# From attention's last out products to the mixer: text order on all engines, the last tile's scores first, a bank for the mask, and tiles taken one at a time

## The chip, the cores and the metric

The kernel runs on one core of a Trainium2 chip. A core has a matrix engine (TensorE, PE in the profile), a vector engine (VectorE, DVE), a scalar engine (ScalarE, ACT), a general engine (GpSimd, POOL) and a queue that issues transfers (SyncE, SP). Each engine works through its own list of instructions in the order in which the program was built, and waits at an instruction until the semaphores named there have been counted up by others. PE writes its results into PSUM, which has eight banks; all else lies in SBUF. The metric is the time of one execution on the device in microseconds (us).

## The reference, cut to what matters

One hybrid layer over x, 4 sequences of 256 positions with 512 channels, that is 1024 rows, in fp32. Four blocks are added to x one after the other, each of which reads a layer-normalised x:

```
x = x + attention(layernorm(x))   # 32 heads of 16, causal, rotary, an adapter prefix
x = x + ffn(layernorm(x))
x = x + mixer(layernorm(x))       # state space: 128 heads of 64, 8 groups
x = x + ffn(layernorm(x))

def ffn(x):                                   # 64 centroids, one assigned to each of 512 outputs
    dots = softmax(x @ centroids.T / 0.1)
    hits = dots > 0.01
    query_sel = any(hits, axis=1)             # by row
    row_sel = any(hits, axis=0)[assignments]  # by output column, over all rows
    return where(query_sel[:, None] & row_sel[None, :], x @ weight.T + bias, 0)

def mixer(x):
    gate, xBC, dt = split(x @ in_proj_w.T)
    xBC = silu(causal_conv(xBC) + conv_b)     # four taps
    y = chunked_scan(xBC, softplus(dt + dt_bias), A, D)
    return (group_rmsnorm(y * silu(gate)) * norm_w) @ out_w.T
```

Which columns the feed-forward adds (`row_sel`) is known only after the last of the eight tiles of 128 rows has its scores; the mixer's normalisation reads x after that.

## The kernel before

x stays in SBUF as eight tiles of 128 rows and 512 channels. Every fp32 product is made of three passes over split operands (`mm3`, lines 110 to 117: high by high, high by low, low by high); a split is a copy on ACT and a subtract on DVE or POOL (L107 and L108). A product of one tile with 512 channels thus takes 4 x 3 passes.

Attention runs tile by tile over four sequences (B = 4), 8 steps of four heads each. Its PSUM pools have 3 (`ps`, all-purpose), 4 (`ps_s`, scores) and 1 bank (`ps_y`). From step 23 on the first feed-forward (`Feed`, lines 175 to 268) is woven in: `fed` normalises a tile, turns it (four PE transposes L166, the split) and multiplies it with the centroids and weights in two halves of 288 columns (`products`); `choice` then makes the hits (max L230, scale L231, exp L233, reciprocal L235, hit L237, running maximum of hits L239), the row's selector `sel` (L243), and the new row (two bias adds L252, then L255, which multiplies by `sel` and adds x).

The attention loop is written in PE's order (`manual_schedule` for PE alone, line 703). On ACT, DVE and POOL a scheduler places the instructions by its own costs. After the last head step the out products of tiles 6 and 7 (`projected_out`, 12 passes of 512 columns each) are made; `finished` adds them to x, takes statistics (L138, L139) and the root (L143, L144). Tiles 6 and 7 are normalised, turned and fed (lines 784 to 806); tile 5's products come between the out products and tile 6's turn.

The mixer begins with `feed.select` (L258): a count product over all hits (L260, L261), a threshold on DVE (L263), a product with the assignment's one-hot (L264) that leaves the mask in PSUM. Then `take` (L268) copies the new row into x where the mask is set, tile by tile. Lines 902 to 929 work in pairs of tiles: two takes, two statistics, one root and one shift (L148) for both, two scalings on ACT (`scale_there`, L153, tile `mxn`), two turns (L166) with splits into `mx` (ACT L107, DVE L108). `normalised(p)` issues for PE: the first quarter of pair p-1, the turns of pair p, the second quarter of pair p-1. A quarter is the product of 256 rows with one weight block: `quarter(0, p)` with the dt weights into `first[0]`, `quarter(1, p)` with the first block of the input projection into `first[1]`. Here too the scheduler places the instructions, except those that are kept in program order (`keep_in_program_order`, the `pin` argument). Two products of x with ones (`warmed`, L122) stand among them on PE.

POOL makes three lower halves of weight splits in this stretch (L108 for `wd` and twice `w`). SP fetches the weights of the projections (`fetch`, L836), and waits there for the splits that free their buffers.

`opening` then makes the step sizes: `dv` (L960) reads `first[0]`, the first convolution (`conv`, L1022) reads `first[1]`, and from there on all engines but SP run in text order (line 1550) for the rest of the kernel: 64 blocks of the mixer, the output products and the second feed-forward.

## Time and profile before

| | |
|---|---|
| median of three runs | 1845.56 us (1845.04, 1845.56, 1850.23) |
| the profiled execution: its time | 1848.5 us |
| its span, first to last instruction | 1846.7 us |
| PE busy | 1779.6 us (96%), 12906 matmuls |
| DVE busy | 1427.2 us (77%) |
| ACT busy | 1283.2 us (69%) |
| POOL busy | 245.5 us (13%) |
| mean granted PE clock | 0.988 |
| first out product of tiles 6 and 7 | 339.83 us |
| first take | 361.80 us |
| `dv`, the first reader of the step sizes' product | 388.37 us |

The profile shows one execution. Busy times of matmuls overlap, because matmuls are pipelined, so PE's 96% is not the share of its peak. A timeline row gives start and length in us, the engine, the line of the program, the operation and out<-in. The chain of work that ended last is followed back from the last instruction, at each step to what released it. The window table gives the busy time of each engine in a stretch, with the number of instructions behind it, in the order PE, weight loads, DVE, ACT, POOL, then the granted PE clock, the share of the transfer engines and GB/s.

### The profile page before, as it was taken

Reading aid. Unit: us, or ns where it says so; the run is one execution under the profiler, and the core shown is the slowest. Engines: PE = TensorE matmul, PEld = TensorE weight load, DVE = VectorE, ACT = ScalarE, POOL = GpSimd, SP = SyncE. Lnnn points to the kernel's source line nnn. Section 1 sums busy time; section 2 is a strip of 40 time slices with the busy share of each in tenths; the row PEclk is TensorE's granted clock in tenths of the full one; section 3 lists DMA queues with packets and bytes.
Section 4 is the critical chain, followed back from the end, with each engine's and each line's share of the span. In section 5 each row is a group of like instructions: output and inputs, shape, how many; then the busy total and the mean of one; then the engine's idle time right before and its main releaser. Section 6 shows DMA issues by size and latency. Waiting matters only on the chain.

```text
span 1846.7 us, 33141 instructions
## 1 busy us (share of the span) xinstructions
PE 1779.6 (96%) x12906; PEld 1451.8 (79%) x12906; DVE 1427.2 (77%) x2152; ACT 1283.2 (69%) x2536; POOL 245.5 (13%) x253
## 2 busy tenths in 40 slices
PE   8999988899999999999999999999999999999988
PEld 6777767677877888888888888888888888888877
DVE  5566667678988777878877787879787878887777
ACT  6666666367778667766866686668667866767664
POOL 6332330000110111101101110110111011101100
PEclk9999989999999999999999999999999999999999
DMA  4000000112325333433442343225333433343321
GB/s 146 1 1 1 23 15 5 47 58 85 103 92 164 100 101 110 133 104 92 131 133 81 108 155 98 98 86 161 96 99 104 154 103 92 114 134 114 96 79 55
DMA packets 134237, 169.45 MB, mean 92 GB/s; under 512 B 12224, under 2 KB 77376, under 8 KB 134080
## 3 DMA queue, kind: packets, MB, share of 16 engines
q1 hardware_dynamic: 125008, 134.30, 24.0%
q10 hardware_dynamic: 9072, 33.03, 4.7%
q8 instruction: 101, 1.65, 0.4%
q14 instruction: 56, 0.46, 0.1%
HBM read 131.64 MB, written 35.65 MB: 91 GB/s over the span
## 4 chain that ended last, share of the span: by engine, by line
PE 79%; ACT 9%; DVE 8%; issue 2%; POOL 1%; DMA 1%; SPq 0%; ACTq 0%; DVEq 0%; POOLq 0%
PE pp L115 13%; PE pp L116 12%; PE pp L117 12%; PE pyy L1145 7%; PE pog L117 6%; PE pog L115 6%; PE pog L116 6%; PE trx L1126 3%; ACT e L502 2%; DVE acc L1033 1%; PE ptr L518 1%; ACT em L1106 1%; PE pq L115 1%; PE pg L1063 1%; PE pq L116 1%
## 5 line engine op out<-in xcount | busy, mean ns | idle before, releaser
L115 PE MATMUL pp<-mx,w 128*128 128x512 f32 (+1 forms) x1160 | 463.6, 400 | 6.9 <-DVE acc L1033 6.2
L117 PE MATMUL pp<-mx,w 128*128 128x512 f32 (+1 forms) x1160 | 452.0, 390 | 0.0
L116 PE MATMUL pp<-mx,w 128*128 128x512 f32 (+1 forms) x1160 | 451.4, 389 | 0.0
L1178 POOL TENSOR_TENSOR sq<-sq,x 128x1024 f32<-128x1024 f32 x54 | 129.8, 2405 | 1204.0 <-ACT x L1177 1204.0
L115 PEld LDWEIGHTS pp<-mx,w 128*128 128x128 f32 x1160 | 218.4, 188 | 52.5 <-issue 7.0
L117 PEld LDWEIGHTS pp<-mx,w 128*128 128x128 f32 x1160 | 218.3, 188 | 46.7 <-DVE w L855 1.2
L116 PEld LDWEIGHTS pp<-mx,w 128*128 128x128 f32 x1160 | 218.7, 189 | 40.7
L1033 DVE SCALAR_TENSOR_TENSOR acc<-pp,cw_s,acc 128x1012 f32<-128x1012 f32 (+2 forms) x192 | 244.7, 1274 | 6.1 <-ACT acc L1022 1.6
L1119 DVE TENSOR_TENSOR em<-em,gm 128x1280 f32<-128x1280 f32 x128 | 189.4, 1489 | 75.3 <-ACT em L1114 75.3
L117 PE MATMUL pog<-wo,gh 128*128 128x512 f32 x512 | 200.1, 391 | 4.2 <-DVE gh L1245 4.2
L115 PE MATMUL pog<-wo,gh 128*128 128x512 f32 x512 | 200.5, 392 | 0.4 <-DVE x L1262 0.4
L116 PE MATMUL pog<-wo,gh 128*128 128x512 f32 x512 | 199.4, 389 | 0.0
L1129 DVE TENSOR_TENSOR xd<-trx,dt_t 128x512 f32<-128x512 f32 x128 | 82.4, 686 | 150.9 <-PE trx L1126 150.9
L1045 ACT ACT_TABLE_LOAD x63 | 80.8, 1283 | 154.6 <-DVE acc L1033 154.5
L1324 ACT ACTIVATE gt<-pp 128x1024 f32<-128x1024 f32 x64 | 65.6, 1026 | 154.2 <-PE pp L117 154.0
L1145 PEld LDWEIGHTS pyy<-em,xd 64*64 64x64 f32 x4096 | 131.7, 135 | 46.2 <-issue 16.9
L1145 PE MATMUL pyy<-em,xd 64*64 64x256 f32 (+3 forms) x4096 | 160.1, 304 | 4.3 <-DVE em L1119 4.3
L1106 ACT ACTIVATE em<-r,end_t 128x128 f32<-128x128 f32 x512 | 163.0, 389 | 0.8
L502 ACT ACTIVATE e<-sc,nmx 128x256 f32<-128x256 f32 (+1 forms) x256 | 104.2, 442 | 21.0 <-DVE nmx L496 20.9
L117 PEld LDWEIGHTS pog<-wo,gh 128*128 128x128 f32 x512 | 96.1, 188 | 26.8 <-DVE gh L1245 6.8
L115 PEld LDWEIGHTS pog<-wo,gh 128*128 128x128 f32 x512 | 96.2, 188 | 20.1 <-issue 0.8
L116 PEld LDWEIGHTS pog<-wo,gh 128*128 128x128 f32 x512 | 96.1, 188 | 19.5
(297 smaller groups left out, 3199.1 us busy)
## 6 DMA issues: line engine op xcount, KB each, us to landing
wr<-in_win_dram SPq DMA_DIRECT2D x144, 256.0 KB, 2.7
r<-cumd SPq DMA_DIRECT2D x256, 128.0 KB, 2.9
spill<-gb ACTq DMA_DIRECT2D x63, 512.0 KB, 3.2
gr<-spill SPq DMA_DIRECT2D x120, 256.0 KB, 3.4
wor<-in_wout_dram SPq DMA_DIRECT2D x64, 256.0 KB, 4.3
out_dram<-x SPq DMA_DIRECT2D x8, 256.0 KB, 2.2
x<-in_x_dram SPq DMA_DIRECT2D x1, 1536.0 KB, 8.8
gr<-spill SPq DMA_DIRECT2D x8, 192.0 KB, 2.5
```

Source lines behind the costliest of these rows:

```text
L115: nc.tensor.matmul(o, lh, rh, start=(first and k == 0), stop=False)
L116: nc.tensor.matmul(o, lh, rl, start=False, stop=False)
L117: nc.tensor.matmul(o, ll, rh, start=False, stop=(last and k == n - 1))
L502: nc.scalar.activation(es_[c][:, 2 * j + pr, :], sc[:, j, :], AF.Exp, bias=nm[:, j : j + 1], accum_out=rs[:, c, h : h + 1],)
L1033: nc.vector.scalar_tensor_tensor(av[:, :, d:], pv[:, :, : L - d], cw_s[:, ch, tap : tap + 1], av[:, :, d:], ALU.mult, ALU.add,)
L1045: nc.scalar.activation(pair(x2).rearrange("p k u i -> p u k i"), acc.rearrange("p (u k i) -> p u k i", u=2, i=Q), AF.Silu,)
L1106: nc.scalar.activation(piece(e, j, c, 2 - c, 2), rv[:, j, 2:, :], AF.Exp, bias=end_t[:, 2 * j + c, h : h + 1],)
L1119: nc.vector.tensor_tensor(e, e, gm, ALU.mult)
L1129: nc.vector.tensor_tensor(xd[:, hs, :].rearrange("p c (h d) -> p c h d", h=2), tr.rearrange("p c (h d) -> p c h d", h=2), dt_t[:, hs, 2 * ...
L1145: nc.tensor.matmul(py[d, u, j * L + c * Q : (j + 1) * L].rearrange("p (k i) -> p k i", i=Q), xd[us, 4 * j + c, d], piece(es2[hh], j, c)[us ...
L1178: (nc.gpsimd if n < NB - 2 else nc.vector).tensor_tensor(sqs[g], sqs[g], x2, ALU.add)
L1324: nc.scalar.activation(gts[i], pp, AF.Silu)
```

## The change

The last two out products go into a new pool of five banks (`f_c`); attention's own PSUM pools are closed ahead of it. The general pool of the mixer (`m_m`, two banks) is opened there already, and one bank (`f_k`) is set apart for the mask; the mixer's two-bank pool `m_y` is opened later for it. From these out products on PE, ACT, DVE and POOL all run in text order, to the end of the kernel.

Tile 5's turn stands ahead of the out products on PE, as before; its products move behind tile 6's turn. Tile 7's first half is split: 64 score columns first, then (behind the mask's products) the other 224 columns and the second half. The square-root table is loaded early by a one-element activation (`primed`), four small products with ones follow the last of PE's fed products, and the two on x go. `select` moves from the mixer to the place after tile 7's hits. The rest of `choice` for tiles 6 and 7 (bias adds, `sel`, L255 of before) is written behind it, and ahead of the first take.

The pairs of tiles are replaced by a loop over single tiles: take and statistics of tile t, root, shift and scaling of tile t-1, turn of tile t-2, and, from t = 4 on, one quarter. There are eight roots and shifts instead of five, and the pins of the pair loop go. The diff, with changes of indentation left out:

```diff
-    def attention(later):
+    def attention(later, region):
         with ExitStack() as es:
-            inner = ExitStack()
+            inner, banks = ExitStack(), ExitStack()
             pool = lambda name, bufs, **kw: es.enter_context(tc.tile_pool(name=name, bufs=bufs, **kw))
...
             p3 = pool("a3", 3)
-            ps = pool("a_m", 3, space=PSUM)
-            ps_s = pool("a_s", 4, space=PSUM)
-            ps_y = pool("a_y", 1, space=PSUM)
+            ps, ps_s, ps_y = (
+                banks.enter_context(tc.tile_pool(name=name, bufs=bufs, space=PSUM))
+                for name, bufs in (("a_m", 3), ("a_s", 4), ("a_y", 1))
+            )
...
-            def projected_out(b, c):
-                po = ps.tile([P, C], F32, name="po", tag="m")
+            def projected_out(b, c, where=None):
+                po = (where or ps).tile([P, C], F32, name="po", tag="c" if where else "m")
                 cs = slice(c * P, (c + 1) * P)
...
                 step("long", n + 2)
-                moved(fed(feed, 5), n)
                 step("turn", n + 2)
-                pos = [projected_out(b, c) for c in range(2)]
-                xns, xss = {}, {}
-                for c, po in enumerate(pos):
-                    t = 2 * b + c
-                    rooted = finished(b, c, po)
+                xs5 = normed(feed.norm, 5)
+                assert not nexts, nexts
+            banks.close()
+            freed = {"reuse_waits": "tile"}
+            mask_at = later.enter_context(tc.tile_pool(name="f_k", bufs=1, space=PSUM, side="right", **freed))
+            ps = ctx.enter_context(tc.tile_pool(name="m_m", bufs=2, space=PSUM, **freed))
+            region.enter_context(tc.manual_schedule(
+                engines={e.engine for e in (nc.tensor, nc.scalar, nc.vector, nc.gpsimd)}
+            ))
+            with tc.tile_pool(name="f_c", bufs=5, space=PSUM, **freed) as ps_c:
+                pos = [projected_out(b, c, ps_c) for c in range(2)]
+                xns, xss, halves = {}, {5: xs5}, {}
+                def added(t):
+                    nc.vector.tensor_tensor(x[:, t, :], x[:, t, :], pos[t - 6], ALU.add)
+                    feed.norm.stats(t)
+                def scaled(t):
+                    feed.norm.root(t, t + 1)
                     xns[t] = p2.tile([P, C], F32, name="axn", tag="t1")
...
-                def turned_late(t):
+                def turned_over(t):
                     tr = ps.tile([P, KC, P], F32, name="tr", tag="m")
-                    xss[t] = [p2.tile([P, KC, P], F32R, name=f"axs{j}", tag=f"axs{j}") for j in range(2)]
-                    feed.norm.turn(xns[t], tr, xss[t])
+                    xss[t] = xs = [
+                        p2.tile([P, KC, P], F32R, name=f"axs{j}", tag=f"axs{j}") for j in range(2)
+                    ]
+                    for k in range(KC):
+                        nc.tensor.transpose(tr[:, k, :], xns[t][:, k * P : (k + 1) * P], ident)
+                    nc.scalar.copy(xs[0], tr)
+                    return lambda: nc.vector.tensor_tensor(xs[1], tr, xs[0].bitcast(F32), ALU.subtract)
-                with tc.issue_after(rooted):
-                    step("long", n + 3)
-                turned_late(TT - 2)
-                halves = {t: [ps_s.tile([P, FH], F32, name="pd", tag="sc") for _ in range(2)] for t in xns}
-                feed.products(xss[TT - 2], 0, halves[TT - 2][0])
-                turned_late(TT - 1)
-                feed.products(xss[TT - 2], 1, halves[TT - 2][1])
-                feed.chosen(TT - 2, halves[TT - 2])
-                feed.tile(TT - 1, xss[TT - 1], halves[TT - 1])
-                assert not nexts, nexts
-            return feed
+                def products(t, j, cols=slice(0, FH)):
+                    if (t, j) not in halves:
+                        halves[t, j] = ps_c.tile([P, FH], F32, name="pd", tag="c")
+                    feed.products(xss[t], j, halves[t, j], cols)
+                added(6)
+                scaled(6)
+                lower = turned_over(6)
+                added(7)
+                lower()
+                scaled(7)
+                primed(AF.Exp)
+                products(5, 0)
+                products(5, 1)
+                c5 = feed.choice(5, [halves[5, j] for j in range(2)])
+                next(c5)
+                lower = turned_over(7)
+                products(6, 0)
+                next(c5)
+                lower()
+                next(c5)
+                next(c5)
+                products(6, 1)
+                products(7, 0, slice(0, NCL))
+                c6 = feed.choice(6, [halves[6, j] for j in range(2)])
+                next(c6)
+                next(c5)
+                halves[7, 1] = ps_c.tile([P, FH], F32, name="pd", tag="c")
+                c7 = feed.choice(7, [halves[7, j] for j in range(2)])
+                next(c7)
+                next(c6)
+                next(c7)
+                primed(AF.Sqrt)
+                cnt = ps.tile([NCL, P], F32, name="cnt", tag="m")
+                feed.select(cnt, mask_at.tile([P, C], F32, name="msk"))
+                products(7, 0, slice(NCL, FH))
+                products(7, 1)
+                warmed(ps.tile([P, C], F32, name="warm", tag="m"), [ones] * 4)
+                for _ in c6:
+                    pass
+                for _ in c7:
+                    pass
+            return feed, ps
-    def mixer(feed, later):
+    def mixer(feed, ps, later):
         with ExitStack() as es, ExitStack() as inner:
...
             po_ = pool("mo", 2, **freed)
-            ps = pool("m_m", 2, space=PSUM, **freed)
             w1 = inside("m1", 1, **freed)
...
             es_y, es_p = ExitStack(), ExitStack()
-            ps_y = es_y.enter_context(tc.tile_pool(name="m_y", bufs=1, space=PSUM, side="right", **freed))
             ps_p = es_p.enter_context(tc.tile_pool(name="m_p", bufs=2, space=PSUM, **freed))
...
             mnorm = Norm("m")
-            feed.select(
-                ps.tile([NCL, P], F32, name="cnt", tag="m"),
-                ps_y.tile([P, B * L], F32, name="msk", tag="pyy")[:, :C],
-            )
             first = [ps_p.tile([P, NT], F32, name="pp", tag="pp") for _ in range(2)]
-            xns = {}
+            xns, parts_ = {}, {}
+            def quarter(j, p):
+                project((wd, pieces[0])[j], first[j], slice(p * L, (p + 1) * L))
-            def normalised(p):
-                quarter = lambda j, n: project((wd, pieces[0])[j], first[j], slice(n * L, (n + 1) * L))
-                if p > 0:
-                    quarter(0, p - 1)
-                if p < B:
-                    for t in (2 * p, 2 * p + 1):
+            for t in range(TT + 2):
+                if t < TT:
+                    feed.take(t)
+                    mnorm.stats(t)
+                if 1 <= t <= TT:
+                    mnorm.root(t - 1, t)
+                    mnorm.shift(t - 1, t)
+                    xns[t - 1] = po_.tile([P, C], F32, name="mxn", tag="wo0", bufs=GB)
+                    mnorm.scale_there(t - 1, xns[t - 1])
+                if t >= 2:
+                    n = t - 2
                         tr = ps.tile([P, KC, P], F32, name="tr", tag="m")
-                        mnorm.turn(xns.pop(t), tr, [v[:, :, t * P : (t + 1) * P] for v in xs])
-                if p > 0:
-                    quarter(1, p - 1)
-            for p in range(B):
-                pin = {"pin": tc.keep_in_program_order} if p else {}
-                ts = (2 * p, 2 * p + 1)
-                if p == 0:
-                    pin = {"pin": tc.keep_in_program_order}
-                    feed.take(0)
-                    mnorm.stats(0, **pin)
-                    feed.take(1, **pin)
-                    for t in ts:
-                        if t:
-                            mnorm.stats(t, **pin)
-                        mnorm.root(t, t + 1)
-                        mnorm.shift(t, t + 1)
-                        warmed(ps.tile([P, C], F32, name="warm", tag="m"), [x[:, t, :]])
-                else:
-                    for t in ts:
-                        feed.take(t, **pin)
-                    for t in ts:
-                        mnorm.stats(t, **pin)
-                    mnorm.root(2 * p, 2 * p + 2)
-                    mnorm.shift(2 * p, 2 * p + 2)
-                if p:
-                    normalised(p - 1)
-                for t in ts:
-                    xns[t] = po_.tile([P, C], F32, name="mxn", tag="wo0", bufs=GB)
-                    mnorm.scale_there(t, xns[t])
-            normalised(B - 1)
-            normalised(B)
+                    mnorm.turn(xns.pop(n), tr, [v[:, :, n * P : (n + 1) * P] for v in xs])
+                    if n >= 2:
+                        quarter(n % 2, n // 2 - 1)
+            for j in range(2):
+                quarter(j, B - 1)
             later.close()
+            ps_y = es_y.enter_context(tc.tile_pool(name="m_y", bufs=1, space=PSUM, side="right", **freed))
             p2 = inside("m2", 2, **freed)
...
-            with tc.manual_schedule(
-                engines={e.engine for e in (nc.tensor, nc.scalar, nc.vector, nc.gpsimd)}
-            ):
                 opening()
...
     later = ExitStack()
-    mixer(attention(later), later)
+    with ExitStack() as region:
+        mixer(*attention(later, region), later)
```

In the diff `opening()` and what follows it lie one level further left than before, and are otherwise the same.

## The prediction

> **What bounds the kernel now.** I read first the page's busy shares and its chain of work that ended last. TensorE (PE) is busy for 96% of the span and holds 79% of the chain, so nearly everywhere the end moves only with PE's work. The change touches one short stretch, from attention's last two out products (339.8 us) to the start of the mixer's step sizes (388.4 us), so I then read the chain, the timeline and the window table of that stretch alone. The chain, start and length in us:
>
> ```profile
> 360.74 0.26 DVE fc L263
> 361.00 0.88 DVE fx L255
> 361.88 0.65 DVE x L268
> ...
> 376.14 0.60 ACT mx L107
> 376.76 0.69 DVE mx L108
> ...
> 380.88 0.69 DVE mx L108
> ...
> 388.37 0.68 ACT dv L960
> ```
>
> The stretch is a relay, not a PE stage. The first take (the predicated copy, L268) follows the last fed tile, then pairs of tiles pass through VectorE (DVE), ScalarE (ACT), PE, ACT and DVE. At full clock one pair costs 380.88 - 376.76 = 4.1 us, two tiles overlapping. The timeline gives the price of each hop:
>
> ```profile
> 361.80 0.71 DVE L268 COPY_PREDICATED x<-msk,fx 128x512 f32<-128x512 uint32 x1
> 362.55 0.69 DVE L138 BATCH_NORM_STATS2 st<-x 128x6 f32<-128x512 f32 x1
> 363.28 0.18 DVE L139 BATCH_NORM_AGGREGATE mmv<-st 128x2 f32<-128x6 f32 x1
> ...
> 382.15 0.15 DVE L144 RECIPROCAL mrs<-mrs 128x2 f32<-128x2 f32 x1
> 382.34 0.16 DVE L148 SCALAR_TENSOR_TENSOR mmv<-mmv,mrs 128x2 f32<-128x2 f32 x1
> ```
>
> Take to statistics is 0.75, statistics to their merge 0.73, reciprocal to shift 0.19. The window table (PE's busy us in each stretch, and PEclk near the end of each row) shows the clock:
>
> ```profile
> 348.70:352.10 3.40, 1.55 (x11) 1.07 (x10) 2.68 (x10) 2.17 (x5) 0.00 (x0) 1.00 0.00 0
> 352.10:355.50 3.40, 3.40 (x17) 3.38 (x16) 1.33 (x5) 0.77 (x3) 0.00 (x0) 0.51 0.00 0
> ...
> 358.90:362.30 3.40, 2.17 (x15) 1.47 (x13) 2.81 (x9) 2.20 (x4) 1.27 (x1) 1.00 0.01 2
> ...
> 365.70:369.10 3.40, 1.21 (x8) 0.73 (x8) 3.31 (x6) 1.90 (x4) 1.18 (x1) 1.00 0.53 151
> 369.10:372.60 3.50, 2.74 (x11) 2.44 (x12) 3.49 (x10) 0.87 (x2) 0.00 (x0) 0.51 0.61 228
> 372.60:376.00 3.40, 3.40 (x18) 3.40 (x18) 0.94 (x3) 0.94 (x2) 0.00 (x0) 0.50 0.00 0
> ```
>
> A stretch with 1.2 to 1.6 us of PE work is followed by one at half clock; 2.17 us kept it full; 2.74 us at half clock did not win it back, 3.40 us did.
>
> **The change, part 1: out products to the first take.** The out products now write into the new pool of five banks. Their first bank is one whose last reader is the yT subtract on L108 (339.70 for 0.41), where PE now waits only for an L252 add that ends at 339.78: +0.3, start 340.15. Start to tile 6's residual add is 3.11 today (339.83 to 342.94), add to its normalised tile's end 2.75 (to 345.69); kept, they put tile 6's turn at 346.05. PE then has no wait: turn 0.44, tile 5's 24 products at 0.133, turn 0.44, tile 6's 24 products, tile 7's 12 score products at 0.111 (the feed-forward at the kernel's end has this shape: 1831.92, 1832.03): 8.6 us, to 354.66. Tile 7's turn is reached at 349.7 and its normalised tile is done near 349.0. This removes what PE loses today: 1.62 us idle before 350.95 and the half-clock row, about 13 products 0.107 us slower each.
>
> The gain is then spent. After the score products land (354.86) come max 0.26, scale 0.27, exp 0.44, reciprocal 0.20, hit 0.28: the second count product at 356.3, its threshold on DVE 0.42 later, mask product 0.34 later, 357.1. PE waits inside this and resumes at 357.4 with 12 products of 224 columns (0.111) and 12 of 288 (0.133): 2.9 us, the last landing at 360.5. On DVE the text puts tile 7's two bias adds and its product with sel ahead of the first take. So a mask ready at 357.5 is not used: bias add 0.50, sel product 0.68, first take 361.7. To this comes GpSimd (POOL). Its three weight splits, now behind an early square-root table load, run about 358 to 361.7, under that last product, which reads two SBUF tiles. Today such an operation takes 0.95 instead of 0.75 beside a split (360.93), and a shift 0.94 instead of 0.16 (365.95). I take +0.4, bounds 0 and 1.3 (one split is 1.27). First take 362.1 against 361.80: **+0.3**, bounds -0.1 and +1.2.
>
> **Part 2: tiles singly, in text order.** In one turn of the new loop DVE's queue holds take(t), statistics, merge, reciprocal and shift of t-1, and the subtract mx1 of t-2; ACT's holds the scaling mxn(t-1), then the copy mx0(t-2). DVE stands at mx1(t-2) for mx0(t-2), which stands on ACT behind mxn(t-1), which waits for DVE's shift(t-1). Behind the waiting subtract stand the next take, statistics and shift. So a turn is a ring: mx1 0.61, take 0.75, statistics 0.73, merge 0.10, reciprocal 0.19, shift to mxn 0.20 (382.34 to 382.54), mxn 0.71 (two in 1.52, 0.81 each), mx0 to mx1 0.62 (376.14 to 376.76): **3.9 us a tile, 7.8 a pair**, against 4.1 now. DVE idles about 1.3 of it.
>
> With T the first take: three takes, statistics and merges, two roots and shifts bring the second shift at T+5.2, the first mx1 at T+6.74 = 368.8 (368.64 now: no loss yet). Today's first pair then costs 8.1 us (368.64 to 376.76), because its products and turns run at half clock; two new turns cost 7.8. The other pairs lose 3.7 each. The sixth mx1 is at T+26.3 = 388.4; the last two tiles have no take in front, and the eighth mx1 comes near T+29.6 = 391.7 against 385.57 now. From the last subtract on the distance to dv is unchanged at full clock (first waiting product 386.31, dv 388.37), as PE does quarter (1, 2) in the meantime. Part 2 without the clock: 391.7 - 385.57 = 6.1, less the 0.3 of part 1: **+5.8**.
>
> Three roots and shifts more (about 0.3 each) lie within these turns. The two 1.1 us warm-up products on x go; four on ones, 0.27 each, stand behind tile 7's products and delay no turn, as the first is due at 366.5. The 12 extra instructions of tile 7's split cost 12 x (0.111 + 0.111 - 0.133) = 1.1 us of PE, counted above. POOL's 0.5 us fill moves behind the splits and nothing waits for it. SP issues the same transfers; the weight fetches that wait for the splits (361.36, 365.68) come 2 to 4 us sooner, and one output-weight fetch goes behind two of them. All had landed long before their readers, which come later now: nothing. The mask's own bank keeps no one waiting.
>
> **Part 3: the clock at the end of the ring.** From the warm-ups (361.5) to the first projection product (about 373) PE has only three turns, so the clock is halved then. Inside the ring one turn at half clock gives PE 12 x 0.213 + 0.8 = 3.4 of 3.9 us, 3.0 per 3.4 us stretch, between the 2.74 that stayed and the 3.40 that recovered. At full clock it gives 2.0, 1.75 per stretch, between the 1.55 that lost and the 2.17 that kept. I take half clock as the likelier, by the nearer row: 1.75 stands closer to 1.55. From 388.4 PE is loaded without a gap: quarter (0, 2), the last turn, then (1, 2), (0, 3), (1, 3). At half clock (0, 2) holds back the last turn by 12 x 0.093 = 1.1, the turn itself takes 0.4 more, and (1, 2) now lies in front of (0, 3). If the clock returns after four to five busy us, dv is **+1.9**; bounds 0 (full clock) and +4.7 (half to the end of (1, 3), where the conv waits).
>
> The Trainium skill's page "TensorE: Matmul & The Clock Gate", section "Why this matters for your kernels", asks for no idle gap over some 3 us, one idle window being what halves the clock. Here a gap of 1.62 us was enough (row 348.70). By the page the ring's 2 us gaps would keep a clock once regained and the sum would be near +6.1; I go by the row.
>
> **Sum.** 0.3 + 5.8 + 1.9 = +8.0 us at dv. From there ACT, DVE and PE follow in one chain, and nothing in the opening waits for anything that did not move (PE's next projection waits for dv itself), so the end moves by as much. The profiled execution took 1848.5 (span 1846.7), 2.9 above the median of the three runs, 1845.56 (1845.04 to 1850.23). Against itself the sum gives 1856.5; by the median, which I forecast, 1853.6.
>
> **Rivals.** (a) *The ring at full clock.* For it: 2.17 us a stretch kept the clock today. Against: 1.75 is less. 0.3 + 5.8 = +6.1: 1851.7. (b) *The head gains more.* If the half-clock row's whole loss (1.4) and the idle 1.62 came off the first take, with the clock as in the forecast: 8.0 - 0.3 - 3.0 = +4.7: 1850.3. Against: the DVE order puts tile 7's adds before the takes. (c) *Not slower: the hops overlap.* If ACT's copies didn't stand behind the scalings, DVE's own work would set the turn: 0.61 + 0.75 + 0.73 + 0.10 + 0.19 + 0.1 = 2.5 us. Five turns save 7.0, at full clock 6.1 - 7.0 = -0.9: 1844.7. It decides below about 2.7 us a turn. For it: the pair at 4.1. Against: both queues' written order. (d) *The change doesn't do what it says*: the mask is early, but no take profits; that lies in the forecast already.
>
> **How the numbers follow.** Forecast (+7 to +11) 0.60; (a) 0.21; (b) 0.11; (c) 0.05; 0.03 for something faster that I do not see. 0.3% is 5.5 us, about what a measurement of this kernel can tell from no change. Slower: 0.60, some 0.15 of (a), 0.04 of (b): 0.79. Same: 0.17. Faster: 0.04. The range takes in (a), the near part of (b), and half clock to the end with the lock (8.0 + 2.8 + 0.9 = +11.7 at most): 1849.8 to 1857.0.
>
> **What would show it.** Subtracts mx1 3.9 us apart, each with some 1.3 us of DVE idle ended by ACT's mx copy; ACT idle ended by the shift; the mask product near 357 and the first take near 362; PEclk near 0.5 after 366; dv near 396. It is wrong if the subtracts stand 2.5 apart, if the first take comes before 360, if PEclk stays at 1.0 through the ring (then rival (a)), or if the chain after dv is shorter than today.

## The result, and the profile after

The changed kernel takes 1858.30 us, median of five executions (1855.83 to 1860.56). The kernel before, on the same chip, now has a median of 1849.57 us over five. The ratio is 1.0053, 95% interval 1.0034 to 1.0072: slower by about half a per cent, 8.7 us between the medians. The profiled execution took 1855.83 us (span 1854.0), against 1848.5 (span 1846.7) for the profile before: 7.3 us.

The forecast was 1853.6, within 1849.8 to 1857.0. The direction and the ring came as told; the time lies above the range.

First the chain of waits of the changed kernel over the stretch (start, length, engine, tile, line):

```profile
360.43 1.47 DVE fx L255
361.89 0.65 DVE x L268
...
371.07 0.81 ACT mxn L153
371.88 0.48 ACT mx L107
...
372.38 0.69 DVE mx L108
373.08 0.65 DVE x L268
...
373.75 0.71 DVE st L138
...
374.93 0.82 ACT mxn L153
...
395.56 1.26 ACT dv L989 x2
```

Scaling, copy, subtract, take, statistics, then (left out here) merge, reciprocal and shift, then the next scaling: the same names come round turn after turn, each once per tile. That is the ring. The timeline shows one turn of it with what each engine waited for:

```profile
372.38 0.69 DVE L108 TENSOR_TENSOR mx<-tr,mx 128x512 fp32r<-128x512 f32 x1 [1.35 <-ACT mx L107]
...
372.99 0.72 DVE L268 COPY_PREDICATED x<-msk,fx 128x512 f32<-128x512 uint32 x1
...
374.74 0.16 DVE L148 SCALAR_TENSOR_TENSOR mmv<-mmv,mrs 128x1 f32<-128x1 f32 x1
...
374.93 0.82 ACT L153 ACTIVATE mxn<-x,mmv,mrs 128x512 f32<-128x512 f32 x1 [2.39 <-DVE mmv L148]
...
375.66 0.56 ACT L107 CAST mx<-tr 128x512 fp32r<-128x512 f32 x1
...
376.25 0.69 DVE L108 TENSOR_TENSOR mx<-tr,mx 128x512 fp32r<-128x512 f32 x1 [1.36 <-ACT mx L107]
```

From subtract to subtract 376.25 - 372.38 = 3.87 us. VectorE stands 1.35 of it, ended by ScalarE's copy; ScalarE stands 2.39, ended by VectorE's shift. Each waits for the other once a turn. In the list of who waited for whom the subtract's line reads (us in all, how often, longest):

```profile
DVE mx L108 <- ACT mx L107: 11.2, 8, 1.7
```

Before, the same wait came twice, 5.6 us in all. The window table (PE's busy us in each stretch first, PEclk as the third figure from the end):

```profile
362.30:365.70 3.40, 0.00 (x0) 0.00 (x0) 3.23 (x9) 0.69 (x2) 0.00 (x0) 0.92 0.84 281
365.70:369.10 3.40, 2.22 (x8) 1.44 (x8) 1.88 (x6) 2.08 (x5) 0.00 (x0) 0.50 0.28 109
...
372.60:376.00 3.40, 3.30 (x17) 2.94 (x16) 2.19 (x6) 1.07 (x2) 0.00 (x0) 0.59 0.00 0
376.00:379.40 3.40, 1.89 (x16) 1.69 (x15) 2.43 (x6) 0.99 (x3) 0.00 (x0) 1.00 0.02 5
...
386.20:389.60 3.40, 1.81 (x11) 1.56 (x12) 1.23 (x6) 2.19 (x4) 0.00 (x0) 0.92 0.00 0
389.60:393.00 3.40, 3.40 (x20) 3.40 (x20) 1.13 (x2) 1.16 (x3) 0.00 (x0) 0.58 0.00 0
```

The clock is halved when PE runs dry behind the head (the part from the out products to the first take). By the means of its rows, 0.59 and 0.92, it comes back near 375.4, holds for some 13 us with 1.8 to 2.4 us of work a stretch, and is lost again near 389, just where PE is loaded at last. So it is neither half all through the ring, as the forecast had it, nor full, as rival (a).

The stretch does not start at the same time in every trace, so all that follows is counted from the start of VectorE's yT subtract on L108, the last operation of attention's heads on VectorE ahead of the out products (339.70 before, 338.90 after). First subtract is the first mx1, last subtract the end of the eighth:

| kernel | first take | first subtract | end of last subtract | dv | time against before, 95% |
|---|---|---|---|---|---|
| before | 22.10 | 28.94 | 46.55 | 48.67 | |
| changed | 22.92 | 29.62 | 54.35 | 56.66 | 1.0053 (1.0034 to 1.0072) |
| changed, again (c1_after) | 22.92 | 29.62 | 53.10 | 55.22 | 1.0041 (1.0028 to 1.0054) |
| e1_order | 23.78 | 30.00 | 51.15 | 53.28 | 1.0036 (1.0024 to 1.0048) |
| e2_pairs | 24.96 | 32.96 | 47.46 | 50.92 | 1.0013 (1.0005 to 1.0022) |
| e3_warm | 23.75 | 30.48 | 54.86 | 56.98 | 1.0052 (1.0038 to 1.0066) |
| e4_early | 18.50 | 28.54 | 52.02 | 54.14 | 1.0037 (1.0024 to 1.0050) |
| e5_fill | 21.67 | 28.38 | 51.86 | 53.98 | 1.0040 (1.0027 to 1.0054) |
| e6_pairs_early | 18.23 | 29.34 | 45.46 | 47.58 | 0.9996 (0.9986 to 1.0006) |
| e7_singles_early | 18.24 | 27.10 | 45.05 | 47.17 | 0.9997 (0.9988 to 1.0005) |
| e8_splits_later | 25.03 | 33.85 | 58.13 | 60.89 | 1.0058 (1.0040 to 1.0077) |
| e9_no_waits | 18.24 | 27.25 | 41.15 | 43.28 | 0.9971 (0.9960 to 0.9983) |
| e10_no_warm | 18.24 | 27.23 | 42.89 | 45.00 | 0.9987 (0.9975 to 0.9998) |
| e11_ring_only | 22.93 | 29.12 | 47.33 | 49.44 | 1.0006 (0.9997 to 1.0015) |

By this count the changed kernel's dv is 56.66 - 48.67 = 7.99 us later; the sum was +8.0. From dv to the end of the span it takes 1458.4 us against 1458.3 before: the rest of the program has not changed.

### The profile page after: what moved, and what is told of

It is laid out like the page before. It is cut to its first block, busy times and chain, and to the rows that moved or that the text cites. A ratio compares the mean times of both kernels' runs of the same rounds, so it can differ in the third digit from the quotient of the medians.

```text
span 1854.0 us, 33179 instructions
## 1 busy us (share of the span) xinstructions
PE 1776.6 (96%) x12922; PEld 1450.1 (78%) x12922; DVE 1430.6 (77%) x2158; ACT 1284.6 (69%) x2541; POOL 245.6 (13%) x253
## 4 chain that ended last, share of the span: by engine, by line
PE 79%; DVE 9%; ACT 8%; issue 2%; POOL 1%; DMA 1%; SPq 0%; ACTq 0%; DVEq 0%; POOLq 0%
PE pp L115 13%; PE pp L117 12%; PE pp L116 12%; PE pyy L1174 7%; PE pog L117 6%; PE pog L115 6%; PE pog L116 6%; PE trx L1155 3%; ACT e L503 2%; DVE acc L1062 1%; PE ptr L519 1%; PE pq L115 1%; ACT em L1135 1%; PE pg L1092 1%; PE pq L116 1%
```

## The experiments

The theory is that of the forecast: the loss is the ring, a little is the head, a little the clock. The rivals: single tiles are dear by themselves; the clock alone is the loss; the text order, by taking the queues from the scheduler, is the loss.

### The ring: the order of four instructions, or pairs

In e1_order the turn is written so that ScalarE copies first and VectorE subtracts last:

```diff
                 if t < TT:
                     feed.take(t)
                     mnorm.stats(t)
+                if t >= 2:
+                    n = t - 2
+                    tr = ps.tile([P, KC, P], F32, name="tr", tag="m")
+                    vs, xn = [v[:, :, n * P : (n + 1) * P] for v in xs], xns.pop(n)
+                    for k in range(KC):
+                        nc.tensor.transpose(tr[:, k, :], xn[:, k * P : (k + 1) * P], ident)
+                    nc.scalar.copy(vs[0], tr)
                 if 1 <= t <= TT:
                     mnorm.root(t - 1, t)
                     mnorm.shift(t - 1, t)
...
                     mnorm.scale_there(t - 1, xns[t - 1])
                 if t >= 2:
-                    n = t - 2
-                    tr = ps.tile([P, KC, P], F32, name="tr", tag="m")
-                    mnorm.turn(xns.pop(n), tr, [v[:, :, n * P : (n + 1) * P] for v in xs])
+                    nc.vector.tensor_tensor(vs[1], tr, vs[0].bitcast(F32), ALU.subtract)
```

> Edit: only the order inside the loop over tiles. ScalarE copies the turned tile (mx0 of t-2) before it scales mxn of t-1, and VectorE subtracts mx1 of t-2 after the shift of t-1, not before the next take. Same instructions, same number. Ring theory (each turn waits for mx0 behind mxn behind the shift, 3.87 us in the changed kernel's trace): the ring is broken, VectorE's own work sets the turn, 0.61 + 0.75 + 0.73 + 0.10 + 0.19 + 0.1 = 2.5 us; with the first mx1 near 367.6, five turns of 2.5 and three shorter ones, and about 1.5 us for a stretch in which TensorE at half clock needs 3.4 us a tile, the eighth mx1 is near 384.5 and dv near 388.5 (395.56 in the changed kernel), so the span is some 7 us shorter, near that of before. Rival, tiles singly are dear by themselves (eight small roots and shifts, single takes): the turn stays above 3.4 us throughout and dv stays above 393. Rival, the clock alone is the loss: the spacing stays near 3.9 with dv near 394.

Measured: turns of 3.23, 3.22, 3.42, then 2.77, 2.76 and 2.76 us. From the first subtract to dv 23.28 us, where the changed kernel took 27.04 and 25.60. dv came to +53.28, 3.4 us earlier than in the changed kernel's first trace, not 7. The ring's idle of 1.35 is gone, so the ring theory holds and both rivals fail (the turn is not above 3.4 throughout, nor near 3.9); but I had put a new wait into the edit. The root of t-1 stands on ScalarE behind the copy of t-2, which waits for PE's turn, so VectorE's reciprocal waits for both, 0.68 to 0.90 us a turn at half clock and 0.22 at full clock. The time, 1854.94 us against 1848.31 before, does not tell this version from the changed kernel: the intervals of their ratios overlap.

e2_pairs writes before's pairs into the changed kernel's text order:

```diff
-            for t in range(TT + 2):
...
+            def turned_pair(p):
+                for n in (2 * p, 2 * p + 1):
+                    tr = ps.tile([P, KC, P], F32, name="tr", tag="m")
+                    mnorm.turn(xns.pop(n), tr, [v[:, :, n * P : (n + 1) * P] for v in xs])
+                if p:
+                    for j in range(2):
+                        quarter(j, p - 1)
+            for p in range(B):
+                ts = (2 * p, 2 * p + 1)
+                for t in ts:
+                    feed.take(t)
+                    mnorm.stats(t)
+                mnorm.root(2 * p, 2 * p + 2)
+                mnorm.shift(2 * p, 2 * p + 2)
+                if p:
+                    turned_pair(p - 1)
+                for t in ts:
+                    xns[t] = po_.tile([P, C], F32, name="mxn", tag="wo0", bufs=GB)
+                    mnorm.scale_there(t, xns[t])
+            turned_pair(B - 1)
```

> Edit: the loop goes over pairs of tiles again (two takes, each with its statistics, one root and one shift for both, then the turns and quarters of the pair before, then the two scalings), written out in text order; head, mask bank and text order of all engines stay as in the changed kernel. Ring theory: here ScalarE has the copies of the pair before ahead of the scalings, so no subtract waits for a scaling of its own turn; VectorE's work sets the pair, 2 x (0.61 + 0.75 + 0.73 + 0.10) + 0.3 = 4.7 us, first mx1 near 368.3, eighth 381 to 384, dv 385.5 to 388.5 against 395.56 in the changed kernel. Rival, the loss comes from taking the queues away from the scheduler, not from single tiles: pairs stay at 7 us or more and dv at 393 or later.

Measured: pairs 5.3 us apart (373.40, 378.69, 383.98), not 4.7; dv at +50.92, which is 5.7 us earlier than in the changed kernel although the first take came 2.0 us later. VectorE also waits 0.36 us a pair for the root. Against the +46.6 to +49.6 expected, dv is late by the 2.0 us of its head, which ran at half clock (see below). The rival that blames the text order is out: pairs did not need 7 us.

e11_ring_only is e1_order without its flaw: the root goes ahead of the copy. Against e1_order:

```diff
                     feed.take(t)
                     mnorm.stats(t)
+                if 1 <= t <= TT:
+                    mnorm.root(t - 1, t)
                 if t >= 2:
...
                     nc.scalar.copy(vs[0], tr)
                 if 1 <= t <= TT:
-                    mnorm.root(t - 1, t)
                     mnorm.shift(t - 1, t)
```

> Edit: the changed kernel with only the ring taken out, as in e7_singles_early: ScalarE does the root of a tile ahead of the copy of the turned tile before it, and that copy ahead of the scaling; VectorE subtracts behind the shift. Single takes, head, mask and splits as in the changed kernel, same number of instructions. Ring theory: turns of 2.4 to 2.9 us in place of 3.87 and 8th subtract 16.5 to 18 us behind the first (24.0 and 22.8 in the two traces of the changed kernel), dv at +48.5 to +51.5 from the yT subtract by how much of the head runs at half clock (+55.2 and +56.7 in the changed kernel, +48.67 before); time 5 to 7 us below the changed kernel's 1857.4 to 1858.3, so 1 to 3 above before. Rival, the ring is worth less than the 5.8 us of the forecast and single takes the rest: turns above 3.2 or dv above +52.5.

The timeline of e11_ring_only, one turn at full clock:

```profile
379.96 0.16 DVE L148 SCALAR_TENSOR_TENSOR mmv<-mmv,mrs 128x1 f32<-128x1 f32 x1
380.04 0.68 DVE L959 TENSOR_TENSOR mx<-tr,mx 128x512 fp32r<-128x512 f32 x1
380.16 0.81 ACT L153 ACTIVATE mxn<-x,mmv,mrs 128x512 f32<-128x512 f32 x1 [0.55 <-DVE mmv L148]
...
381.72 0.59 ACT L953 CAST mx<-tr 128x512 fp32r<-128x512 f32 x1 [0.56 <-PE tr L952]
...
382.47 0.68 DVE L959 TENSOR_TENSOR mx<-tr,mx 128x512 fp32r<-128x512 f32 x1
```

The subtracts at 380.04 and 382.47 stand behind no wait: 2.43 us a turn, VectorE's own work; the turns before, some at half clock, took 2.44 to 3.10. First take and head are those of the changed kernel to 0.01 us (+22.93). dv comes at +49.44, 7.2 and 5.8 us earlier than in the two traces of the changed kernel, and the time is 1850.10 us where the kernel before has 1850.06: ratio 1.0006 (0.9997 to 1.0015). With the same single takes, the same mask and the same head, the order of root, copy, scaling and subtract alone makes the loss go away. This settles the ring, and that single tiles cost next to nothing.

### The clock

e3_warm fills PE's idle time with products that nobody reads:

```diff
+                if t == 2:
+                    warmed(first[1][:, 3 * L :], [ones] * 16)
...
                         quarter(n % 2, n // 2 - 1)
+                    if n < 7:
+                        warmed(first[1][:, 3 * L :], [ones] * (2, 9, 4, 4, 4, 4, 4)[n])
```

> Edit: products of ones with ones (0.26 us each, no reader) fill TensorE's idle time in the ring: 16 before the first turn, 2, 9 and then 4 behind the following turns. Order of everything else as in the changed kernel. Theory (ring of 3.87 us on VectorE and ScalarE, clock a smaller term): granted clock 1.0 throughout from 362 to 396, spacing of the subtracts unchanged at 3.8 to 3.9, only the end gains: quarter and turn behind 389 are at full clock, dv 1.2 to 1.6 us earlier, 394.0 to 394.4. Rival, half clock sets the turn (12 x 0.213 + 0.8 = 3.4 of 3.9): spacing falls below 3.6 and dv comes before 393.

The window table of e3_warm:

```profile
365.70:369.10 3.40, 1.82 (x15) 1.44 (x13) 2.58 (x9) 1.61 (x3) 0.00 (x0) 1.00 0.34 124
369.10:372.60 3.50, 2.67 (x22) 2.48 (x22) 2.41 (x6) 1.04 (x4) 0.00 (x0) 1.00 0.00 0
```

At full clock the subtracts are still 3.87 us apart (369.88, 373.75): the rival that half clock sets the turn is out. dv was to come at 394.0 to 394.4 and came at 396.38 (+56.98). Two things ate the gain. The head lost its clock in this execution (first take +23.75). And my own four products behind quarter (0, 2) stood in front of the last turn: ScalarE waited 1.41 us for it. The clock also fell to 0.65 between 376 and 379.4 in spite of the filling. As a measure of the clock's price the run is not clean.

c1_after, the changed kernel unaltered, turned out to measure it.

> The changed kernel once more, unaltered, to see what repeats. In its first trace PE waits 1.22 and 0.38 us around the count products (354 to 356.4) and keeps full clock; in the traces of e1_order, e2_pairs, e3_warm and e4_early, whose head up to there has the same instructions in the same order, the same wait is followed by about 3.4 us at half clock, and the first take comes 23.8 us and more behind the yT subtract in place of 22.92. Theory: the wait stands near the limit of the clock gate, so an execution of the changed kernel pays 0.8 to 2 us in its head or doesn't; this trace shows half clock between 352 and 363 and a first take at +23.7 to +25, and the ring again at 3.87 a tile. Rival, the experiments' edits behind the head cause it: this trace shows PEclk 1.00 there and a first take at +22.9.

Head and ring repeat to 0.01 us: first take +22.92, first subtract +29.62, turns of 3.87 and 3.88. So my theory on the head was wrong for this execution: the clock stayed at 1.00 there. The ring's clock differs; the window table of c1_after:

```profile
379.40:382.80 3.40, 2.46 (x15) 1.92 (x13) 2.42 (x6) 1.00 (x4) 0.00 (x0) 0.77 0.00 0
382.80:386.20 3.40, 3.27 (x16) 3.27 (x16) 2.42 (x6) 1.00 (x4) 0.00 (x0) 0.50 0.00 0
386.20:389.60 3.40, 3.20 (x20) 2.74 (x20) 0.94 (x4) 2.51 (x5) 0.00 (x0) 0.73 0.00 0
```

Here the clock was lost near 381, inside the ring where PE has slack, and was back near 388, early in quarter (0, 2). In the first trace it was lost at 389. From first subtract to dv c1_after takes 25.60 us, the first trace 27.04. The traces of e4_early and e5_fill, with full clock at the end, take 25.60 too. So the clock's term is 1.44 us where the loss falls on the end, and nothing where it falls into the ring.

e10_no_warm is e9_no_waits (below) without its filling, and so a clean pair with it:

```diff
-                warmed(ps.tile([P, C], F32, name="warm", tag="m"), [ones] * 14)
+                warmed(ps.tile([P, C], F32, name="warm", tag="m"), [ones] * 4)
...
-                    if p == 1:
-                        warmed(first[1][:, 3 * L :], [ones] * 12)
```

> Edit: e9_no_waits with 4 products of ones in place of 14 behind tile 7's products and none in place of 12 behind the first pair's turn; all else the same. Theory (the clock term is real, but only where TensorE is near the path): PEclk falls to 0.5 between 360 and 376 as in e6_pairs_early; the second pair's products and turns then take 24 x 0.213 + 1.7 = 6.8 us against VectorE's 4.3, so the third pair's subtracts come 1.5 to 3 us later than in e9_no_waits and dv stands at +44.8 to +46.5 from the yT subtract (+43.28); span 1.5 to 3.2 us above that of e9_no_waits. Rival, VectorE alone sets the stretch: dv within 0.5 us of e9_no_waits whatever the clock.

The window tables, first of e9_no_waits, then of e10_no_warm:

```profile
365.70:369.10 3.40, 2.11 (x18) 1.91 (x17) 3.33 (x8) 1.42 (x3) 1.56 (x2) 1.00 0.63 193
369.10:372.60 3.50, 3.22 (x27) 2.97 (x26) 3.40 (x10) 2.08 (x5) 0.00 (x0) 1.00 0.91 333
```

```profile
365.70:369.10 3.40, 1.40 (x5) 1.11 (x6) 3.29 (x10) 1.18 (x3) 2.12 (x2) 0.50 0.51 160
369.10:372.60 3.50, 3.50 (x18) 3.50 (x18) 2.26 (x7) 1.54 (x3) 0.00 (x0) 0.50 0.93 321
```

Without the filling VectorE is busy 2.26 us in a stretch in which it was busy 3.40: it waits 1.17 and 0.16 us for copies of turns that PE makes at half clock. dv stands at +45.00 against +43.28: 1.7 us, as expected. Where no ring is in the way, the clock costs.

### The head

e5_fill moves one line:

```diff
+                products(7, 1)
                 feed.select(cnt, mask_at.tile([P, C], F32, name="msk"))
                 products(7, 0, slice(NCL, FH))
-                products(7, 1)
```

> Edit: one line moves. Tile 7's second half of products (12 of 288 columns, a bank of its own) stands in TensorE's order ahead of the count and mask products, not behind them; the loop over tiles is the changed kernel's. Theory (the wait at the count costs the clock): TensorE has no wait of more than 0.4 us there, PEclk stays 1.00 up to the warm-ups, the mask lands at most 0.4 us later than in the changed kernel's trace, the first take comes 22.2 to 22.9 us behind the yT subtract, ring unchanged at 3.87; span 0.5 to 2 us below the changed kernel's in the same call. Rival, the half clock comes from elsewhere: it appears again in the same place, first take at +23.7 or later.

Measured: first take +21.67, 1.25 us earlier than in the changed kernel and a little before the expected 22.2; ring 3.87 as before; dv +53.98. The medians, 1856.78 and 1857.42 for c1_after beside it, differ by less than they scatter, so the time does not confirm it; the trace does. These 1.25 us are not the clock's, which those traces of the changed kernel kept too: tile 7's product with sel starts 0.64 us earlier and takes 0.85 us in place of 1.47. What the wait at the count can do to the clock shows elsewhere. First the wait, in the changed kernel, which kept the clock, and in e8_splits_later (below), which has the same order on PE and lost it:

```profile
355.29 0.40 PE L260 MATMUL cnt<-ones,fh 128*64 128x128 f32 x2 [1.22 <-DVE fse L235]
```

```profile
357.07 0.40 PE L260 MATMUL cnt<-ones,fh 128*64 128x128 f32 x2 [1.22 <-DVE fse L235]
```

Then the window tables around the count; first e5_fill, then e8_splits_later:

```profile
352.10:355.50 3.40, 3.40 (x30) 3.40 (x29) 2.42 (x7) 0.41 (x2) 0.00 (x0) 1.00 0.00 0
355.50:358.90 3.40, 3.02 (x22) 2.39 (x21) 1.99 (x11) 2.45 (x6) 0.00 (x0) 1.00 0.01 2
358.90:362.30 3.40, 2.42 (x20) 2.23 (x20) 3.33 (x6) 0.99 (x2) 3.38 (x3) 1.00 0.31 79
```

```profile
355.50:358.90 3.40, 1.80 (x10) 0.93 (x10) 2.33 (x11) 1.89 (x4) 0.00 (x0) 0.87 0.01 2
358.90:362.30 3.40, 3.40 (x16) 3.40 (x17) 1.27 (x3) 0.00 (x0) 0.00 (x0) 0.50 0.00 0
```

The head with the wait at the count is in eight traces: the changed kernel, c1_after, e11_ring_only, e1_order, e2_pairs, e3_warm, e4_early and e8_splits_later. In the first three the clock stayed full, in the other five it was halved right there. Where it stayed the first take comes at +22.92; where it fell, and takes are not moved, at +23.75, +23.78, +24.96 and +25.03. The filled head is in five traces (e5, e6, e7, e9, e10) and kept the clock there in all five. Five of eight against none of five supports that the wait causes the loss, on few traces; what decides it from one execution to the next stays open.

e8_splits_later moves the three weight splits from ahead of the loop into its second turn:

```diff
-            split(wd, wdt_s, nc.gpsimd)
-            prepare(0)
-            prepare(1)
...
+                if t == 1:
+                    split(wd, wdt_s, nc.gpsimd)
+                    prepare(0)
+                    prepare(1)
```

> Edit: the three weight splits (ScalarE casts, GpSimd subtracts) move in the text from ahead of the loop into its second turn, behind the first scaling; all else is the changed kernel. Theory (GpSimd's subtracts hold up VectorE's products with sel: 1.83 and 1.47 us in both traces of the changed kernel beside them, 0.74 alone): the two L255 take 0.75 to 0.85, the first take comes 1.0 to 1.8 us sooner, 21.1 to 21.9 us behind the yT subtract in place of 22.92; the splits then run beside the ring, where VectorE idles 1.35 us a turn, at the cost of one or two shifts of 0.9 in place of 0.16; dv at +53.5 to +55.5 (+55.2 and +56.7 in the two traces). Rival, the 1.83 and 1.47 come from something else (TensorE's products or the reads of PSUM): they stay above 1.2 and the first take at +22.5 or later.

Timeline of the changed kernel, VectorE's products with sel, then GpSimd's subtracts:

```profile
357.14 1.83 DVE L255 SCALAR_TENSOR_TENSOR fx<-fx,fsel,x 128x512 f32<-128x512 f32 x1
...
360.43 1.47 DVE L255 SCALAR_TENSOR_TENSOR fx<-fx,fsel,x 128x512 f32<-128x512 f32 x1
```

```profile
357.12 1.30 POOL L108 TENSOR_TENSOR wd<-wdt_s,wd 128x512 fp32r<-128x512 f32 x1 [38.18 <-DVE fx L252]
358.38 2.96 POOL L108 TENSOR_TENSOR w<-wr,w 128x512 fp32r<-128x512 f32 x2
```

And of e8_splits_later:

```profile
358.93 0.75 DVE L255 SCALAR_TENSOR_TENSOR fx<-fx,fsel,x 128x512 f32<-128x512 f32 x1
...
365.03 0.75 DVE L255 SCALAR_TENSOR_TENSOR fx<-fx,fsel,x 128x512 f32<-128x512 f32 x1
```

Both take 0.75 us when GpSimd is still, so the stretching by GpSimd is shown. The expected gain in the first take did not come: the clock was halved in this head, tile 7's last products ended at 364.5, and the take waited for them (+25.03). Then the splits, pushed into the ring, hit a shift there (1.11 us in place of 0.16) and held the root back behind the casts. Its dv is the latest of all and its ratio, 1.0058, the highest; what the splits cost in the head, about 0.7 us by the last product's 1.47 - 0.75, is argued from the trace and was not seen in a time.

e4_early lets two tiles use the early mask:

```diff
+                feed.mnorm = Norm("m")
+                for t in range(2):
+                    feed.take(t)
+                    feed.mnorm.stats(t)
                 for _ in c6:
                     pass
...
-                if t < TT:
+                if 2 <= t < TT:
```

> Edit: takes 0 and 1, each with its statistics, stand in VectorE's queue right behind the mask product's two bias adds of tile 6, ahead of tile 6's product with sel and tile 7's adds and product with sel; the loop has the other six takes as before. Same instructions. Theory (the early mask, 356.4 in the changed kernel, gains nothing only because four VectorE operations of tiles 6 and 7 stand ahead of the first take): first take near 357.2 instead of 361.82, third take near 362.6 instead of 365.19, first mx1 near 366.2 instead of 368.52, ring unchanged at 3.87 a tile, dv near 393.2 (395.56). Rival, GpSimd's weight splits, 357.1 to 361.3, are the head's limit whatever stands there: takes and statistics between 357 and 361 take 1.2 to 1.8 us each in place of 0.7, and the first mx1 comes no sooner than 367.8.

Measured: first take +18.50, 4.4 us earlier, takes of 0.75 and 0.70 us beside GpSimd (so that rival is out); third take +25.21 against +26.29, first subtract +28.54 against +29.62. The gain is 1.1, not 2.3, as tile 7's products ran at half clock and its product with sel moved to 364.47. So the early mask was there for the taking, as rival (d) said, but two takes in front of the ring only move the ring.

### Versions without the ring

e6_pairs_early and e7_singles_early join the filled head, an early first pair, and turns without a ring, once by pairs and once singly:

```diff
+                feed.mnorm = Norm("m")
+                for t in range(2):
+                    feed.take(t)
+                for t in range(2):
+                    feed.mnorm.stats(t)
+                feed.mnorm.root(0, 2)
+                feed.mnorm.shift(0, 2)
                 for _ in c6:
                     pass
```

In the mixer e7 has the loop of e11_ring_only for tiles 2 to 7, and e6 goes over pairs:

```diff
+            for p in range(B):
+                ts = (2 * p, 2 * p + 1)
+                if p:
+                    for t in ts:
+                        feed.take(t)
+                    for t in ts:
+                        mnorm.stats(t)
+                    mnorm.root(2 * p, 2 * p + 2)
+                    mnorm.shift(2 * p, 2 * p + 2)
+                    if p > 1:
+                        quarter(0, p - 2)
+                    turned(p - 1)
+                    if p > 1:
+                        quarter(1, p - 2)
+                for t in ts:
+                    xns[t] = po_.tile([P, C], F32, name="mxn", tag="wo0", bufs=GB)
+                    mnorm.scale_there(t, xns[t])
```

> Edit: e5_fill, and the first pair's takes, statistics, root and shift stand right behind the mask, ahead of the rest of tiles 6 and 7 on VectorE; the other pairs as in e2_pairs but with both takes ahead of both statistics and with a quarter of the projection on either side of each pair's turns. Theory: with no ring and no wait behind the mask VectorE's work alone sets the stretch: 3.4 us for the first pair, 3.0 for tiles 6 and 7, then 4.1 to 4.5 a pair; last subtract near 41.5 to 45 us behind the yT subtract and dv at +44 to +47.5, against +48.67 in the kernel before and +56.66 in the changed one: span 1 to 5 us below the kernel before. Rival, TensorE's half clock or the last pair's own relay sets the end: dv at +48 or later, no gain on the kernel before.

> Edit: the head of e6_pairs_early, but the other six tiles singly as in e1_order, with ScalarE's root of a tile ahead of the copy of the turned tile before it (in e1_order it stood behind, and VectorE's reciprocal waited for it). Same instructions as the changed kernel but for one root and shift less. Theory: single tiles cost nothing by themselves once no engine waits in a ring: turns of 2.5 to 2.8 us, dv at +45 to +48.5 from the yT subtract, within 1.5 us of e6_pairs_early. Rival, single tiles are dear: turns over 3.2 us at full clock and dv 3 us or more behind e6_pairs_early.

Measured: dv at +47.58 and +47.17, 9 us earlier than in the changed kernel and 1.1 and 1.5 earlier than before; times 1848.17 and 1847.72 against 1848.01, no difference that can be told. Singles are level with pairs (turns of 2.41 to 2.87 us), so singles are not dear. e6 stands just beyond its expected +44 to +47.5: the weight casts slid in front of its first scaling, and the clock was halved from 363 to 376.5.

e9_no_waits removes what was left. Both subtracts of a pair stand ahead of the next reciprocal, the splits stand behind the first scalings, and PE is filled:

`turned` now leaves the subtracts out and gives back its tiles, and `lowered` subtracts. Against e6_pairs_early:

```diff
-                warmed(ps.tile([P, C], F32, name="warm", tag="m"), [ones] * 4)
+                warmed(ps.tile([P, C], F32, name="warm", tag="m"), [ones] * 14)
...
                     for t in ts:
                         mnorm.stats(t)
-                    mnorm.root(2 * p, 2 * p + 2)
-                    mnorm.shift(2 * p, 2 * p + 2)
                     if p > 1:
                         quarter(0, p - 2)
-                    turned(p - 1)
+                    trs = turned(p - 1)
+                    if p == 1:
+                        warmed(first[1][:, 3 * L :], [ones] * 12)
                     if p > 1:
                         quarter(1, p - 2)
+                    lowered(trs)
+                    mnorm.root(2 * p, 2 * p + 2)
+                    mnorm.shift(2 * p, 2 * p + 2)
                 for t in ts:
...
                     mnorm.scale_there(t, xns[t])
+                if p == 0:
+                    split(wd, wdt_s, nc.gpsimd)
+                    prepare(0)
+                    prepare(1)
```

In the head the two bias adds of tile 6 stand between the first pair's statistics and its reciprocal.

> Edit: e6_pairs_early, and (1) the weight splits move behind the first pair's scalings as in e8_splits_later, (2) the two subtracts of a pair stand ahead of the next pair's reciprocal and shift, so that VectorE does not wait for ScalarE's root, (3) 14 products of ones in place of 4 behind tile 7's products and 12 behind the first pair's turn keep TensorE busy. Theory (VectorE's own work is the floor of the stretch): first scaling near +22.5 from the yT subtract (+23 in e6_pairs_early), PEclk 1.00 to the end, pairs of 4.2 to 4.6 us, last subtract near +40 to +42, dv at +42.5 to +45.5 against +48.67 in the kernel before: span 3 to 6 us below the kernel before. Rival, the last relay or half clock takes it back: dv at +47 or later, as in e6_pairs_early and e7_singles_early, and no gain that a measurement can tell.

Its timeline, one pair:

```profile
370.74 1.26 DVE L962 TENSOR_TENSOR mx<-tr,mx 128x512 fp32r<-128x512 f32 x2
...
372.10 0.16 DVE L148 SCALAR_TENSOR_TENSOR mmv<-mmv,mrs 128x2 f32<-128x2 f32 x1
372.17 1.37 DVE L268 COPY_PREDICATED x<-msk,fx 128x512 f32<-128x512 uint32 x2
372.29 1.52 ACT L153 ACTIVATE mxn<-x,mmv,mrs 128x512 f32<-128x512 f32 x2 [1.15 <-DVE mmv L148]
...
374.09 1.07 ACT L956 CAST mx<-tr 128x512 fp32r<-128x512 f32 x2 [0.28 <-PE tr L955]
```

The next pair of subtracts starts at 375.04: 4.30 us a pair, and VectorE has no wait in it. dv is at +43.28, 5.4 us before that of the kernel before, and the time is 1844.08 us against 1849.33: ratio 0.9971 (0.9960 to 0.9983). So with the ring out of the way a version with the early mask and the text order is faster than the kernel before. How much of the gain is the early mask, the text order or the later splits no run takes apart; the filling of PE alone is 1.7 of the 5.4 us, by e10_no_warm.

## Why the prediction was right and wrong

**The ring** (+5.8 of the sum) was right in place, size and cause: 3.9 us a tile forecast, 3.86 to 3.88 measured, VectorE idle 1.35 for the 1.3 told, ended by the copy. Taking it out (e11_ring_only) gave back 5.8 us at dv against c1_after and 7.2 against the first trace; the 7.2 hold 1.44 us of clock besides.

**The head** (+0.3, bounds -0.1 and +1.2): +0.8 with the clock kept, within the bounds, low by half a us, mostly since the last product with sel took 1.47 beside the splits and the +0.4 for them was short by 0.3. Where the clock fell and takes were not moved, in four of the versions, the head cost +1.7 to +2.9, beyond the upper bound. What was wrong is "PE waits inside this and resumes at 357.4": the wait was counted in time and not in clock, although the same text quotes a row in which a wait of 1.62 us before halved it. The two traces of the changed kernel kept the clock there, so this is not shown to have made its time longer.

**The clock at the ring's end** (+1.9, bounds 0 and +4.7): 1.44 in the first trace, 0 in the second, both within the bounds. The argument behind it, half clock throughout because 1.75 us a stretch is nearer 1.55, was wrong: the clock came back at the first quarter, held at 1.8 to 2.4 us a stretch, and fell again later. That the size was nearly right in the first trace is luck. So is the match of that trace's whole, +7.99, with the sum of +8.0: the head was half a us too low and the clock half a us too high. The second trace gives +6.55.

The Trainium skill's page "TensorE: Matmul & The Clock Gate", section "Why this matters for your kernels", warns only of idle gaps of PE over some 3 us; by it the clock, once regained, would have held through the ring. It did not: the longest idle of PE between 376 and 389 was 1.81 us in the first trace and 1.79 in the second, and the clock fell in both. In e4_early and e5_fill, with the same ring and gaps of up to 1.81 and 1.80 us, it held to the end. So the row with the gap of 1.62 us was the better guide only in telling that the clock may fall.

**The base** is the step that failed: it put the time above the range. "Against itself the sum gives 1856.5; by the median, which I forecast, 1853.6": the median of three, 1845.56, was a lucky one. In 70 later executions the kernel before has a median of 1849.0 (1844.17 to 1854.52), and 6 of the 70 were as quick as 1845.56. 1849.0 + 8.0 = 1857.0, and the ten executions of the changed kernel have a median of 1857.6. Both ends of the range stood on the same base and so were 3.4 us too low; nothing in it allowed for the base itself. On 1849.0 the same range runs from 1853.2 to 1860.4, and 1858.30 lies inside. The shift was forecast at +8.0; between these medians it is 8.6.

**The rivals.** (a) full clock in the ring: half true, as the two traces show; it gives +6.1, and c1_after stands at 55.22 - 48.67 = +6.55. (b) the head gains more: no, it lost. (c) hops that overlap: not in this order, but with the order changed the turn is 2.4 us, dv 0.8 us later than before and the time the same, where -0.9 was worked out. (d) no take profits from the early mask: true, and e4_early and e9_no_waits show that the takes could.

What stays open: the medians differ by 8.6, the traces by 7.3 (first) and 5.1 (second, 1851.8 against 1846.7). Heads that lose their clock may account for some of it, but this is not shown: no trace of the unaltered changed kernel caught one.

## What to carry to other kernels

When loops over engines are written in text order, draw the ring: for each engine, the instruction that stands at the head of its queue, and what its releaser stands behind. A copy on one engine and the subtract that waits for it on another should be split, so that the copying engine issues first what is ready (here the old tile's copy before the new tile's scaling), and the waiting subtract goes last in its turn, with nothing due behind it. And a forecast in absolute time needs a base with its own spread: here three executions were off by 3.4 us, two fifths of the effect.

## What was not expected of the hardware

- **The scatter goes with the clock.** Sorted by the mean granted clock of each execution, the 70 of the kernel before have medians of 1845.6 us at 0.991 (5 of them), 1847.8 at 0.989 (16), 1849.9 at 0.987 (12) and 1852.3 at 0.985 (4). Some 1.1 us goes with each thousandth.
- **A wait of 1.22 us can cost the clock, or not.** The same instructions with the same wait kept it in three traces and lost it in five, and PE's next products then ran at half speed for several us.
- **GpSimd stretches some of VectorE's work and not the rest.** Beside a weight split the product with sel, which reads two tiles of SBUF, takes 1.83 and 1.47 us in place of 0.75, and a shift 1.11 in place of 0.16. Takes (0.75 and 0.70) and statistics do not change. GpSimd's own two splits take 2.96 in place of 2.49.

The Trainium skill's page "SBUF — State Buffer", section "SBUF: two separate sides", puts this down to a lock on a pair of ports that VectorE's operations with two inputs from SBUF contend for with GpSimd. The runs agree: 1.83 and 1.47 us beside a split, 0.75 without one.
